# Layer 2 projections of a two-layer cross-attention packed to 320 columns, with high and low halves side by side in the third block

## The chip, the cores and the metric

The kernel runs on one core of a Trainium2 chip. The core has a matrix engine (PE, with its weight loads shown apart as PEld), a vector engine (DVE), a scalar engine (ACT), GpSimd (POOL), and SyncE (SP), which here issues nearly all transfers (DMAs). The metric is the device time of one execution in microseconds (us), lower is better. The kernel before has a median of 1475.77 us over 3 runs (1475.01 to 1476.06).

## The reference, cut to what matters

Two cross-attention layers run one after the other on 16 samples of 256 positions and 320 channels, with 20 heads of 16 channels. The context has 252 text positions used by layer 2 (77 by layer 1) and image tokens behind them. Layer 2 is this:

```python
q = heads(hidden_states @ W_q)
k_t = heads(text_ehs @ W_k)
v_t = heads(text_ehs @ W_v)
scores_t = jnp.einsum('bhsd,bhtd->bhst', q, k_t) * attn_scale
probs_t = jax.nn.softmax(scores_t, axis=-1)
...
k_ip = heads(ip_ehs @ W_k_ip)
attn_scores = jnp.einsum('bhsd,bhnd->bhsn', q, k_ip) * attn_scale
qsem = _l2norm(jnp.einsum('bhst,bte->bhse', probs_t, text_ehs))
fused = attn_scores + SEM_SCALE * jnp.einsum('bhse,bne->bhsn', qsem, ip_n)
probs_ip = jax.nn.softmax(fused, axis=-1) * spatial_mask[None, None, :, None]
out = (text_out + IP_SCALE * ip_out) @ W_out + b_out + residual
```

What is touched here is how `q`, `k_t` and `k_ip` of layer 2 are computed and how they reach the scores.

## The kernel before, in words

**Precision by halves.** A float32 value is held as a high half, rounded to the type that PE multiplies (`FR`), and a low half, the rest. A product is three matmuls per 128 rows of contraction: high by high, high by low, low by high (`prod`). Copies that make the high half are on ACT, the subtractions that make the low half on DVE or POOL (`halves`).

**Projections of layer 2.** `keys1(b)` computes the keys of sample b: the weights `w1["k"]` (tile wA) are 512 rows by `CP` = 384 columns, which are 16 channels of 24 heads, 4 of them padding; three blocks `m` of 128 columns are made, each by 12 matmuls of 252 moving columns (tile cta is the context). `queries(1, a)` does the same for the queries through `project` (weights in tile wE, input halves in tile hq): three blocks of 8 matmuls of 256 moving columns, fewer than nine since the contraction is 320 long and the last 64 rows of it carry high and low halves of the input side by side.

**The way to the scores.** The halves of the keys (tile kst) and of the queries (tile q) are written to DRAM, `kd` and `qd`, as three planes (low, high, high and high, low, high), so that one contraction over 48 rows (3 planes by 16 channels) gives the three products of a head's score. `stacks1(k)` reads them back per group of four heads as stacks of 48 rows (tiles ks and qs, two heads above one another at rows 0 and 64), with one further row of -1 against the row maxima. PE multiplies the stacks twice: L922 gives scores (tile S) for the maxima and L917 the transposed scores (tile T) that are exponentiated.

**Order.** The program is written as slots: 80 of layer 1 (five groups of four heads for each of 16 samples), then 80 of layer 2. `slot1(k)` has the transposed scores of group k, the scores of group k+2, the value product of k-2 (L988, L990), and the normalizing product of k-1 (`norm1`, L975: 14 matmuls of 512 moving columns, tiles ctb and gm). All else (projections, context loads, output) is cut into steps, and a table `STEPS` gives the due time of each in slots; `fill(now)` runs the steps that are due where a slot yields a number. In layer 2 the order of PE, ACT, DVE and POOL is the written one; SP's order of DMAs is set by a scheduler. Each engine works through its queue in order, so on SP a DMA that waits holds those behind it.

**Weights.** `weights7` loads the layer 2 key weights for text and image tokens, `weights2` the query weights, `weights8` clears a table in DRAM. They run during the last slots of layer 1.

The rows of the profile name tiles without numbers. The lines to follow: L260 and L632 (matmuls of the projections), L562 and L564 (key halves), L640 and L641 (query halves), L83 (every SP DMA), L917, L922 (scores), L975 (`norm1`).

```python
def slot1(k):
    yield lambda: both1(k, 1)
    if last:
        yield lambda: norm1(last, 0, 0)
    yield 0.2
    for parts in summed:
        yield lambda: settle1(*parts)
```

Of the kernel before, what the change touches and what calls it, by code (L numbers as in the profile page):

```python
# [16 lines left out]
B = 16  # L17
S = 256
H = 20
# [13 lines left out]
KS0 = 127  # L33
KS1 = 49
XROW = 48


# [12 lines left out]
def xattn2(  # L50
# [100 lines left out]

    kd = [dram.tile([B // 2, 3, CQ, 2, S], F32, name="kd0"), dram.tile([B, 3, CP, 1, S], F32, name="kd1")]
    vipd = dram.tile([BI, CP], F32, name="vipd")
# [79 lines left out]

    def weights(w_d, tag, half=None, wait=0, raw="raw"):

        w, parts, view = by_row(w_d, tag)
        yield from in_turn(parts, wait, raw)
        if half is not None:
            nc.vector.tensor_scalar_mul(w[:, 1, 2], f(w[:, 1, 2]), half)
        return view  # L240
# [14 lines left out]
    def prod(out, lhs, rhs, kt):  # L255

        terms = [(k, a, b) for k in range(kt) for a, b in ((0, 0), (0, 1), (1, 0))]
        first = last = None
        for i, (k, a, b) in enumerate(terms):
            last = mm(out, lhs(a, k), rhs(b, k), start=i == 0, stop=i == len(terms) - 1)  # L260
            first = first or last
        return first, last

    def context(b, n, wait=0):
# [94 lines left out]

    def last_keys(ct, kst, jobs):  # L360
# [119 lines left out]
    def weights7():  # L480
        cip = w1["cip"]
        image, wki1 = by_column(wki1_d)
        _, text, w1["k"] = by_row(wk1_d, "wA")
        yield from in_turn(image + text, 0.3, "rawc")
        for m in range(3):
            kp = bank()[:, :BI]
            prod(kp, lambda s, k: wki1(s, k, slice(m * 128, m * 128 + 128)), lambda s, k: cip[:, s, k], 4)
            halves(kip[:, 0, m], kip[:, 1, m], kp)
            yield
# [25 lines left out]
    def weights2():  # L515
        wq.append((yield from weights(wq1_d, "wE", tmask[:, 3:4], 0.3, "rawc")))

# [3 lines left out]
    def weights8():  # L521

        zero = buf("kb", [128, 3, 2, 96], FR, bufs=2, name="zero").rearrange("p a b c -> p (a b c)")
        nc.gpsimd.memset(f(zero), 0.0)
        yield
        for b in range(0, B, 4):
# [26 lines left out]
    def keys1(b):  # L553
        ct = ct1[b] = yield from context(b, 1, 0.3)
        for m in range(3):
# [7 lines left out]
            late(  # L563
                lambda kst=kst, kp=kp: nc.vector.tensor_sub(kst[:, 1, 0, :T1], kp, f(kst[:, 0, 0, :T1])),  # L564
                lambda kst=kst, m=m: keys_out(kd[1][b], m, kst),
            )
# [58 lines left out]

    def project(l, w, a, evac):

        terms = [(s, k, t) for k in range(2) for s, t in ((0, k), (0, 3 + k), (1, k))] + [(0, 2, 2), (1, 2, 2)]
        for m in range(3):
            pp = bank()[:, :S]  # L630
            for i, (s, k, t) in enumerate(terms):
                mm(pp, w(s, k, slice(m * 128, (m + 1) * 128)), a[:, t], start=i == 0, stop=i == len(terms) - 1)  # L632
            evac(m, pp)
            yield

    def queries(l, a):
# [5 lines left out]

        yield from project(l, wq[l], a, evac)
        qd = dram.tile([3, (CQ, CP)[l], S], F32, tag=f"qd{l}", name=f"qd{l}", bufs=2)
        settled()
        if l:
            for r, s in ((0, 0), (1, 1), (2, 0)):
                dma(qd[r].rearrange("(m p) t -> p m t", p=128), qh[:, s])
        else:
# [97 lines left out]
    def stacks1(k):  # L747
# [7 lines left out]
        for u in range(2):  # L755
            rows = slice(64 * u, 64 * u + XROW)
            hs = slice(4 * g + u, 4 * g + u + 3, 2)
            if k - NS < n:
                dma(K[64 * u + XROW : 64 * u + KS1], w1["ind"])
            dma(K[rows], stack_rows(kd[1][b][:, :, 0])[:, hs])  # L760
            dma(Q[rows], stack_rows(qd)[:, hs])

# [140 lines left out]
    def both1(k, t):  # L903
# [14 lines left out]
        if a:  # L918
            for j in range(2):
                for u in range(2):  # L920
                    rows = slice(64 * u, 64 * u + XROW)
                    mm(sp[:, 2 * u + j], a[0][rows, j, t * 128 : (t + 1) * 128], a[1][rows, j], start=True, stop=True)  # L922
# [28 lines left out]
    def maxima1(k):  # L951
# [5 lines left out]
        nc.scalar.copy(mt, mp[:4, :S])  # L957
        row = QK[k][0].rearrange("(u p) j t -> u p j t", u=2)[:, XROW]
        late(lambda: nc.scalar.dma_start(f(row), f(mt)))
# [33 lines left out]
    def slot1(k):  # L993
# [10 lines left out]
        yield release  # L1004
        yield lambda: both1(k, 1)
        if last:
            yield lambda: norm1(last, 0, 0)
        yield 0.2
        for parts in summed:
# [170 lines left out]
    def first_keys():  # L1180
# [5 lines left out]
    STEPS = {  # L1186
        "k1": (-7, -6.2, -6.2, -5, -4.2, -3.4,),
        "t1": (-3.2, -2.2, -2.2, -1.4, -0.2,),
        "o1": (-7, -6.8, -6, -5.8, -4, -3.4,),
        "i1": (6.8, 7.6, 7.6, 8.8, 9.4, 9.6, 10.6, 10.8, 10.8, 12.2,),  # L1190
        "c1": (12.8, 12.8, 13.4, 14, 14, 15.8,),
        ("i1", B - 2): (6.6, 7, 7.2, 7.2, 7.8, 8, 8.6, 9.2, 9.2, 9.6,),
        ("c1", B - 2): (9.8, 11.8, 11.8, 12.2, 12.4, 12.4,),
        ("i1", B - 1): (6.8, 7.6, 7.8, 10, 10, 10, 11, 11, 11.2, 12,),
        ("c1", B - 1): (12.2, 13, 13, 13.2, 13.4, 16,),
# [30 lines left out]
    }  # L1226
    def first(n, *key_times):
# [242 lines left out]
```

## Time and profile before

| what | before |
|---|---|
| median of the runs | 1475.77 us |
| the profiled execution, its own time | 1477.49 us |
| its span, first to last instruction | 1475.7 us |
| PE busy | 1433.6 us (97%) |
| PE weight loads busy | 1186.7 us (80%) |
| DVE busy | 1166.0 us (79%) |
| POOL busy | 1151.8 us (78%) |
| ACT busy | 956.5 us (65%) |
| PE clock granted, mean | 0.993 |

The profile is one execution. Its parts used here are the busy shares, the chain that ended last, the waits of PE, busy times in chosen stretches, and the instructions in order of time. An engine at 97% busy is not proof that it bounds the kernel, since the ends of matmuls are modelled; the distances from one matmul's start to the next one's start are recorded, and are the firmer reading.

### The profile page before, as it was taken

How to read it: one execution, taken by the hardware profiler on the slowest of the kernel's cores; microseconds unless marked ns; L12 is line 12 of the kernel's file. 1: busy time of each engine (PE TensorE's matmuls, PEld its weight loads, DVE VectorE, ACT ScalarE, POOL GpSimd, SP SyncE). 2: the span in 40 equal slices, each digit the busy share in tenths (PEclk: the TensorE clock that was granted, in tenths of full speed). 3: DMA queues.
4: the chain of work that ended last, by engine and by line, in shares of the span. 5: the costliest groups of instructions: out<-in, count | busy, mean ns of one | idle time of the engine just before them, and what ended most of it. 6: DMA issues, size and time to landing. Idle time of an engine off the chain costs nothing.

```text
span 1475.7 us, 35302 instructions
## 1 busy us (share of the span) xinstructions
PE 1433.6 (97%) x12438; PEld 1186.7 (80%) x12438; DVE 1166.0 (79%) x2569; ACT 956.5 (65%) x2074; POOL 1151.8 (78%) x1173
## 2 busy tenths in 40 slices
PE   6899999999999999799999999999999999999998
PEld 6788888888888878687778887888888888888865
DVE  5487676777677787967888888888888888888897
ACT  5577676767676776756666566656665666566553
POOL 4179797979797877987788877787778877887785
PEclk9999999999999999999999999999999999999999
DMA  6756565656656577565434433543354345433511
GB/s 196 194 160 184 134 184 141 184 143 165 162 154 164 144 195 205 140 184 158 138 102 140 146 119 101 161 146 102 118 161 146 89 131 161 135 101 116 150 32 50
DMA packets 230667, 211.78 MB, mean 144 GB/s; under 512 B 56314, under 2 KB 217116, under 8 KB 230492
## 3 DMA queue, kind: packets, MB, share of 16 engines
q1 hardware_dynamic: 229222, 208.56, 50.3%
q8 instruction: 99, 1.62, 0.5%
q10 hardware_dynamic: 1270, 0.98, 0.2%
q14 instruction: 76, 0.62, 0.1%
HBM read 122.07 MB, written 86.44 MB: 141 GB/s over the span
## 4 chain that ended last, share of the span: by engine, by line
PE 86%; DMA 4%; DVE 3%; POOL 3%; ACT 2%; issue 1%; SPq 0%; ACTq 0%; DVEq 0%; POOLq 0%
PE X L260 22%; PE X L975 18%; PE X L632 11%; PE P L833 7%; PE S L772 5%; PE P L988 5%; PE T L917 5%; PE T L795 4%; PE S L922 3%; PE P L990 2%; DMA kd<-kst 2%; PE X L1108 1%; POOL P L801 1%; PE X L690 1%; POOL wt L966 1%
## 5 line engine op out<-in xcount | busy, mean ns | idle before, releaser
L801 POOL TENSOR_TENSOR P<-P,rs 128x512 f32<-128x512 f32 x320 | 413.6, 1316 | 140.2 <-ACT P L798 140.2
L975 PE MATMUL X<-ctb,gm 128*128 128x512 f32 x1120 | 295.3, 407 | 0.0
L966 POOL TENSOR_TENSOR wt<-P,ctb 128x512 f32<-128x512 f32 x212 | 268.6, 1296 | 0.0
L923 DVE TENSOR_REDUCE mn<-S 128x4 fp32r<-128x1008 f32 x160 | 192.8, 1205 | 81.0 <-PE S L922 79.4
L975 PEld LDWEIGHTS X<-ctb,gm 128*128 128x128 f32 x1120 | 203.6, 190 | 49.4 <-issue 0.4
L798 ACT ACTIVATE P<-T 128x512 f32<-128x512 f32 x320 | 174.7, 593 | 100.5 <-PE T L795 81.0
L978 DVE TENSOR_TENSOR wt<-X,wt 128x512 f32<-128x512 f32 x240 | 159.3, 681 | 4.9 <-PE X L975 4.9
L929 ACT ACTIVATE P<-T 128x512 f32<-128x512 f32 x212 | 115.0, 597 | 54.5 <-PE T L917 41.6
L980 POOL TENSOR_TENSOR wt<-wt 128x512 f32<-128x512 f32 x80 | 103.6, 1295 | 58.3 <-DVE wt L978 58.3
L965 ACT ACTIVATE ctb<-P 128x512 fp32r<-128x512 f32 x212 | 122.5, 625 | 32.7 <-PE X L975 31.1
L774 DVE TENSOR_REDUCE mn<-S 128x4 fp32r<-128x716 f32 x160 | 142.4, 890 | 0.0
L833 PE MATMUL P<-P,vr 128*32 128x256 f32 x1920 | 123.8, 387 | 1.8 <-DVE tmp L850 0.8
L632 PE MATMUL X<-hq,wE 128*128 128x256 f32 x768 | 111.1, 289 | 4.4 <-ACT hq L615 3.9
L260 PE MATMUL X<-cta,wA 128*128 128x252 f32 (+3 forms) x726 | 104.2, 289 | 6.9 <-ACT wA L187 6.8
L632 PE MATMUL X<-ho,wF 128*128 128x256 f32 x768 | 106.6, 284 | 0.9 <-DVE ho L871 0.6
L632 PEld LDWEIGHTS X<-hq,wE 128*128 128x128 f32 x768 | 101.6, 195 | 7.2 <-ACT hq L615 4.4
L260 PEld LDWEIGHTS X<-cta,wA 128*128 128x128 f32 (+1 forms) x726 | 94.4, 191 | 10.7 <-ACT wA L187 7.0
L632 PEld LDWEIGHTS X<-ho,wF 128*128 128x128 f32 x768 | 98.7, 189 | 3.9 <-DVE ho L871 1.0
L844 DVE STREAM_TRANSPOSE nt<-P 128x512 f32<-128x512 f32 x80 | 57.0, 713 | 44.2 <-PE P L833 43.9
L773 DVE TENSOR_REDUCE mn<-S 128x4 fp32r<-128x308 f32 x160 | 74.5, 466 | 21.5 <-PE S L772 21.1
L833 PEld LDWEIGHTS P<-P,vr 128*32 128x32 f32 x1920 | 55.7, 110 | 42.7 <-issue 6.0
L772 PE MATMUL S<-ks,qs 125*128 125x256 f32 x480 | 87.0, 304 | 0.9 <-DVE mn L774 0.8
(223 smaller groups left out, 3279.7 us busy)
## 6 DMA issues: line engine op xcount, KB each, us to landing
qd<-q SPq DMA_DIRECT2D x48, 384.0 KB
kd<-kst SPq DMA_DIRECT2D x66, 256.0 KB
rawc<-in_cT_dram SPq DMA_DIRECT2D x60, 256.0 KB
qs<-qd SPq DMA_DIRECT2D x160, 96.0 KB
ks<-kd SPq DMA_DIRECT2D x160, 96.0 KB
qs<-qd SPq DMA_DIRECT2D x60, 192.0 KB
ks<-kd SPq DMA_DIRECT2D x60, 192.0 KB
qd<-q SPq DMA_DIRECT2D x32, 256.0 KB
```

The costliest lines, as they stand in the source:

```text
L260: last = mm(out, lhs(a, k), rhs(b, k), start=i == 0, stop=i == len(terms) - 1)
L632: mm(pp, w(s, k, slice(m * 128, (m + 1) * 128)), a[:, t], start=i == 0, stop=i == len(terms) - 1)
L772: mm(sp[:, h], Q[: XROW + T0, h, t * 128 : (t + 1) * 128], K[: XROW + T0, h], start=True, stop=True)
L774: anchor(nc.vector.tensor_reduce(mn[:, t, 1], sp[:, :, T0:], axis=AX.X, op=ALU.max))
L798: exp = anchor(nc.scalar.activation(pt, st[p], AF.Exp, scale=SCALE))
L801: anchor(nc.gpsimd.tensor_mul(pt, pt, rs[:, t : t + 1].to_broadcast([128, 2, S])))
L833: mm(pv[32 * s : 32 * s + 32, o : o + S], v[:, vt, h : h + 32], P[k, s // 2][:, t, s % 2], start=vt < 2, stop=vt != 1,)
L923: anchor(nc.vector.tensor_reduce(maxes[k + 2][:, t], sp[:, :, :T1], axis=AX.X, op=ALU.max))
L965: nc.scalar.activation(R[k, u][:, t], P[k, u][:, t], AF.Copy, scale=0.5)
L966: anchor(nc.gpsimd.tensor_sub(W[k, u][:, t], P[k, u][:, t], f(R[k, u][:, t])))
L975: mm(yp, gm[:, gb], R[k, u][:, kt], start=i == 0, stop=i == len(blocks[n]) - 1)
L978: nc.vector.tensor_mul(product, yp, w[:, n])
```

## The change

The layer 2 weights for keys, image keys and queries are packed to `CQ` = 320 columns (16 channels of 20 heads). Blocks 0 and 1 (256 columns) are computed as before. The third block has 64 columns left; the high halves of these weights fill its left 64 columns, and their low halves are copied beside them into the right 64 (`lows_beside`, on POOL). One matmul then gives both, so the third block takes 8 matmuls for keys (`both_halves`: context high and low) and 5 for queries, and the part that came from the low weights stands in rows 64 to 127 of the result as remainder rows.

The remainders are not added to the main rows. They enter the scores as further rows of the stacks: four rows in which the remainder of the query meets the main key, and four in which the main query meets the remainder of the key, so a stack has 56 rows (`X1`) in place of 48. The first of each four is only partly used (64 columns are 3.2 channels of 20 heads), and the unused parts in DRAM are cleared once, in `weights8`. The buffers `qd1` in DRAM become two fixed tensors.

For each sample the queries are now written by 7 DMAs (before 3) and the third key block by 4 (before 2). The image key weights come in four loads of 128 rows (before three loads of 128 columns). Further, `norm1(last, 0, 0)` moves behind the first `yield 0.2` of a slot, and due times in `STEPS` move by some tenths of a slot; the entries added for the last samples of layer 1 repeat what the default gave.

```diff
+    def lows_beside(w):
+        nc.gpsimd.tensor_copy(w[:, 0, :, CQ:], f(w[:, 1, :, LAST]))
...
+    def both_halves(out, lhs, rhs, kt):
+        for k in range(kt):
+            for s in range(2):
+                mm(out, lhs(k), rhs(s, k), start=k + s == 0, stop=k + s == kt)
...
+    def keys1_out(d, m, kst):
+        hi, lo = kst[:, 0, 0], kst[:, 1, 0]
+        n, lo_row = min(CQ - m * 128, 128), m * 128
+        planes = d[:EXTRA].rearrange("(r c) t -> c r t", c=CQ)[lo_row : lo_row + n]
+        dma(planes[:, 1:], hi[:n].unsqueeze(1).to_broadcast([n, 2, S]))
+        dma(planes[:, 0], lo[:n])
+        if m == 2:
+            dma(d[EXTRA + H - 4 : EXTRA + 4 * H], hi[:64])
+            dma(d[EXTRA + 5 * H - 4 : EXTRA + 8 * H], hi[64:])
...
-            prod(kp, lambda s, k: w1["k"](s, k, ms), lambda s, k: ct(s, k)[:, :T1], 4)
+            if m < 2:
+                prod(kp, lambda s, k: w1["k"](s, k, ms), lambda s, k: ct(s, k)[:, :T1], 4)
+            else:
+                both_halves(kp, lambda k: w1["k"](0, k, ms), lambda s, k: ct(s, k)[:, :T1], 4)
...
+            chain = [(0, k, t) for s, k, t in terms if s == 0] if beside and m == 2 else terms
...
             for r, s in ((0, 0), (1, 1), (2, 0)):
-                dma(qd[r].rearrange("(m p) t -> p m t", p=128), qh[:, s])
+                dma(planes[: 2 * 128, r].rearrange("(m p) t -> p m t", p=128), qh[:, s, :2])
+            dma(planes[LAST, ::2], qh[:64, 0, 2].unsqueeze(1).to_broadcast([64, 2, S]))
+            dma(planes[LAST, 1], qh[:64, 1, 2])
+            dma(qd[EXTRA + H - 4 : EXTRA + 4 * H], qh[64:, 0, 2])
+            dma(qd[EXTRA + 5 * H - 4 : EXTRA + 8 * H], qh[:64, 0, 2])
...
+        if last:
+            yield lambda: norm1(last, 0, 0)
-        yield 0.2
...
-        "k1": (-7, -6.2, -6.2, -5, -4.2, -3.4,),
+        "k1": (-7, -6.2, -6.2, -5.2, -4.2, -3.6,),
```

Two places show what this makes of the order. The first is PE in a slot of layer 2 in the middle of the program, between the scores of one slot and those of the next: the rows with cta,wA at 252 columns are the third key block, those with ctb,gm are `norm1`, those with wC,cta make values. Before:

```order
L922 MATMUL S<-ks_190,qs_186 128x256 x4
L975 MATMUL X<-ctb_82,gm 128x512 x7
L975 MATMUL X<-ctb_83,gm 128x512 x4
L260 MATMUL X<-cta_80,wA_84 128x252 x6
L260 MATMUL X<-cta_81,wA_84 128x252 x6
L975 MATMUL X<-ctb_83,gm 128x512 x3
L260 MATMUL X<-wC_155,cta_80 128x320 x6
L260 MATMUL X<-wC_155,cta_81 128x320 x6
L955 MATMUL X<-ident_r,mn_555 4x128 x2
```

And now:

```order
L969 MATMUL S<-ks_192,qs_188 128x256 x4
L1022 MATMUL X<-ctb_84,gm 128x512 x7
L279 MATMUL X<-cta_82,wA_86 128x252 x4
L279 MATMUL X<-cta_83,wA_86 128x252 x4
L1022 MATMUL X<-ctb_85,gm 128x512 x7
L271 MATMUL X<-wC_157,cta_82 128x320 x6
L271 MATMUL X<-wC_157,cta_83 128x320 x6
L1002 MATMUL X<-ident_r,mn_557 4x128 x2
```

Four matmuls are gone, and the third key block stands four matmuls of 512 columns further ahead.

The second is SP's queue for one sample, from the writes of its queries to the reads of its key stacks (qd and kd are the DRAM buffers; out_dram and xc belong to another sample's output). Before:

```order
L83 DMA out_dram<-xc_747 128x3x256
L83 DMA qd_12911<-q_297 128x3x256 x2
L83 DMA xc_747<-x1d 128x3x256
L83 DMA qd_12911<-q_297 128x3x256
L83 DMA kd_67<-kst_236 128x2x256
L83 DMA kd_67<-kst_236 128x256
L83 DMA qs_186<-qd_12911 48x2x256 x4
L83 DMA qs_187<-qd_12911 48x2x256 x2
L83 DMA kd_67<-kst_235 128x2x256
L83 DMA kd_67<-kst_235 128x256
L83 DMA qs_187<-qd_12911 48x2x256 x2
L83 DMA ks_190<-kd_67 48x2x256 x4
```

And now, where the writes of query blocks 0 and 1 (128x2x256, three of them) and the first of the third block (64x2x256) already stand ahead of these rows:

```order
L86 DMA qd_68<-q_299 64x256 x2
L86 DMA out_dram<-xc_749 128x3x256
L86 DMA qd_68<-q_299 64x256
L86 DMA kd_67<-kst_238 128x2x256
L86 DMA kd_67<-kst_238 128x256
L86 DMA xc_749<-x1d 128x3x256
L86 DMA qs_188<-qd_68 56x2x256 x4
L86 DMA qs_189<-qd_68 56x2x256 x2
L86 DMA kd_67<-kst_237 64x2x256
L86 DMA kd_67<-kst_237 64x256 x3
L86 DMA qs_189<-qd_68 56x2x256 x2
L86 DMA ks_192<-kd_67 56x2x256 x4
```

The last query write moved ahead of the load of xc, and the third key block has four writes instead of two between the query stacks and the key stacks.

More of the change, by code (lines that the diff above doesn't have):

```diff
@@ L33 @@
 KS0 = 127
-KS1 = 49
+KS1 = 57
 XROW = 48
+X1 = 56
+LAST = slice(2 * 128, CQ)
+EXTRA = 3 * CQ
 SIZES = dict(RAW=2, KST=2, NP=4, NR=4, CTA=2, CTB=2, WB=4, M=2)
@@ L150, in const_tile @@
         return const.tile(shape, dtype, tag=tag, name=tag)
-    kd = [dram.tile([B // 2, 3, CQ, 2, S], F32, name="kd0"), dram.tile([B, 3, CP, 1, S], F32, name="kd1")]
+    kd = [dram.tile([B // 2, 3, CQ, 2, S], F32, name="kd0"), dram.tile([B, X1 * H, S], F32, name="kd1")]
+    qd1 = [dram.tile([X1 * H, S], F32, name=f"qd1{i}") for i in range(2)]
     vipd = dram.tile([BI, CP], F32, name="vipd")
@@ L232, in by_column, with weights @@
         )
-    def weights(w_d, tag, half=None, wait=0, raw="raw"):
-        w, parts, view = by_row(w_d, tag)
+    def lows_beside(w):
+        nc.gpsimd.tensor_copy(w[:, 0, :, CQ:], f(w[:, 1, :, LAST]))
+    def weights(w_d, tag, half=None, wait=0, raw="raw", beside=False):
+        w, parts, view = by_row(w_d, tag, beside)
         yield from in_turn(parts, wait, raw)
         if half is not None:
-            nc.vector.tensor_scalar_mul(w[:, 1, 2], f(w[:, 1, 2]), half)
+            n = CQ if beside else CP
+            nc.vector.tensor_scalar_mul(w[:, 1, 2, :n], f(w[:, 1, 2, :n]), half)
+        if beside:
+            lows_beside(w)
         return view
@@ L515, in weights2 @@
     def weights2():
-        wq.append((yield from weights(wq1_d, "wE", tmask[:, 3:4], 0.3, "rawc")))
+        wq.append((yield from weights(wq1_d, "wE", tmask[:, 3:4], 0.3, "rawc", True)))
     def weights4(l):
@@ L524, in weights8 @@
         nc.gpsimd.memset(f(zero), 0.0)
+        blank = zero[:16, :S].unsqueeze(1)
+        for d in (*(q.unsqueeze(0) for q in qd1), kd[1]):
+            for row in (EXTRA, EXTRA + 4 * H):
+                dma(d[:, row : row + 16].rearrange("b p t -> p b t"), blank.to_broadcast([16, d.shape[0], S]))
         yield
@@ L624, in split, with project @@
         return hl
-    def project(l, w, a, evac):
+    def project(l, w, a, evac, beside=False):
         terms = [(s, k, t) for k in range(2) for s, t in ((0, k), (0, 3 + k), (1, k))] + [(0, 2, 2), (1, 2, 2)]
@@ L630, in project @@
             pp = bank()[:, :S]
-            for i, (s, k, t) in enumerate(terms):
-                mm(pp, w(s, k, slice(m * 128, (m + 1) * 128)), a[:, t], start=i == 0, stop=i == len(terms) - 1)
+            chain = [(0, k, t) for s, k, t in terms if s == 0] if beside and m == 2 else terms
+            for i, (s, k, t) in enumerate(chain):
+                mm(pp, w(s, k, slice(m * 128, (m + 1) * 128)), a[:, t], start=i == 0, stop=i == len(chain) - 1)
             evac(m, pp)
             yield
+    opened = []
     def queries(l, a):
```

47 lines of the change are left out of this document (31 added, 16 removed), and 24 rows, old and new, of the table STEPS.

## The prediction

> **What bounds the kernel now.** I read the page's busy shares first, then its chain that ended last, then PE's waits in layer 2, then PE row by row.
>
> ```profile
> PE 1433.6 (97%) x12438; PEld 1186.7 (80%) x12438; DVE 1166.0 (79%) x2569; ACT 956.5 (65%) x2074; POOL 1151.8 (78%) x1173
> PE 86%; DMA 4%; DVE 3%; POOL 3%; ACT 2%; issue 1%; SPq 0%; ACTq 0%; DVEq 0%; POOLq 0%
> ```
>
> PE is 97% busy and 86% of the chain. Since a busy PE can still be a slow one, the next rows matter more: stretches in us, each with the busy us (and instructions) of PE, PEld, DVE, ACT and POOL, then granted clock, DMA share and GB/s. The first is one sample of layer 2 (49.65 us, from one read of the same table to the next), the second the slot in it with the third key block; then come all waits of PE between 760 and 1440 us.
>
> ```profile
> 1001.30:1050.95 49.65, 49.65 (x419) 40.23 (x418) 42.55 (x90) 30.88 (x68) 39.46 (x44) 1.00 0.43 129
> 1028.10:1035.49 7.39, 7.39 (x53) 6.45 (x50) 6.84 (x15) 4.04 (x9) 5.38 (x9) 1.00 0.72 228
> ```
>
> ```profile
> PE P L990 <- DVE wt L980: 1.1, 1, 1.1
> PE S L922 <- DVE sr L939: 0.9, 2, 0.7
> ```
>
> In 680 us PE waits 2.0 us. DVE has 42.55 of 49.65 us, POOL 39.46. PE in order of time (start, us, group) says whether it runs at its own pace:
>
> ```profile
> 1011.08 1.11 PE L632 MATMUL X<-hq,wE 128*128 128x256 f32 x8
> 1012.03 2.49 PE L975 MATMUL X<-ctb,gm 128*128 128x512 f32 x10
> ...
> 1028.10 0.40 PE L922 MATMUL S<-ks,qs 48*128 48x256 f32 x4
> 1028.43 2.83 PE L975 MATMUL X<-ctb,gm 128*128 128x512 f32 x11
> 1031.10 1.55 PE L260 MATMUL X<-cta,wA 128*128 128x252 f32 x12
> 1032.48 0.86 PE L975 MATMUL X<-ctb,gm 128*128 128x512 f32 x3
> ...
> 1035.49 0.41 PE L922 MATMUL S<-ks,qs 48*128 48x256 f32 x4
> ```
>
> From start to start, 11 matmuls of 512 columns take 2.67 us (243 ns each), 12 of 252 columns 1.38 us (115 ns), 8 of 256 columns 0.95 us (119 ns). The time goes with the columns, there is no gap between groups, and so a matmul taken out of layer 2 gives back its own start-to-start time, as long as no other engine steps in.
>
> **The removed matmuls.** Each of 16 samples loses 4 of 252 columns and 3 of 256: 4 x 0.115 + 3 x 0.119 = 0.817 us, so 13.1 us in all. The other price for the same instructions is busy time by group:
>
> ```profile
> L632 PE MATMUL X<-hq,wE 128*128 128x256 f32 x768 | 111.1, 289 | 4.4 <-ACT hq L615 3.9 <-DVE hq L616 0.3
> L260 PE MATMUL X<-cta,wA 128*128 128x252 f32 x576 | 75.8, 279 | 0.2 <-POOL cta L188 0.2
> ```
>
> 111.1/768 = 145 ns and 75.8/576 = 132 ns, which make 0.96 us a sample and 15.4 us. I take 13.1, since busy time counts the tails of matmuls that overlap the next group; 15.4 is the upper end.
>
> By the Trainium skill (TensorE: Matmul & The Clock Gate, Back-to-back issue gap) an isolated matmul takes N/2.4 + 2.5 ns, which as an estimate makes 12.1 us here; the same section's sustained figure of about 131 ns at 512 columns would make the rest cheaper still, near 11 us. The 243 ns above contradict that sustained figure, and the trace stands.
>
> The score matmuls contract 56 or 57 rows instead of 48 or 49. Their moving columns stay 256, and the rows above show that 48 contracted rows take 0.33 us for four (1028.10 to 1028.43) with two heads above one another; 57 rows still fit into the same 64. Cost nothing.
>
> **The moved norm1 and steps.** These reorder PE work without changing it. What could be lost is cover. In the slot of the third key block DVE is busy 6.84 of 7.39 us; the slot shrinks by 4 x 0.115 = 0.46 us to 6.93, so DVE still fits with 0.09 us to spare. DVE at the end of that slot (start, us, group, and in brackets the idle time before):
>
> ```profile
> 1035.11 0.44 DVE L1100 STREAM_TRANSPOSE rs<-rs 128x256 f32<-128x256 f32 x1
> 1035.93 1.21 DVE L923 TENSOR_REDUCE mn<-S 128x4 fp32r<-128x1008 f32 x1 [0.38 <-PE S L922]
> ```
>
> DVE idles 0.38 us there and then reduces the scores; behind this reduction waits the next write of S on PE, the half of the scores about 2.1 us on, and the reduction needs 1.21 of these. So a DVE that is 0.1 us late holds nobody. If that cover were gone in full, the loss is bounded by the saving of that slot: 16 x 0.46 = 7.4 us. I take 0.
>
> **DMAs.** A sample issues 46 DMAs on SP in place of 40 (queries 7 for 3, third key block 4 for 2), and the stacks carry 56 rows for 48. Bytes have room: the DMA share in the sample's row is 0.43. What counts is the time at which the first key stacks of the next sample land. SP (start, us for all issues of the row):
>
> ```profile
> 1029.58 0.36 SPq L83 DMA_DIRECT2D xc<-x1d  x1
> 1030.03 0.44 SPq L83 DMA_DIRECT2D qd<-q  x1
> 1030.57 1.45 SPq L83 DMA_DIRECT2D kd<-kst  x2
> 1034.40 2.82 SPq L83 DMA_DIRECT2D qs<-qd  x6
> 1037.33 0.89 SPq L83 DMA_DIRECT2D kd<-kst  x2
> ...
> 1040.69 4.06 SPq L83 DMA_DIRECT2D ks<-kd  x8
> 1044.85 0.38 SPq L83 DMA_DIRECT2D sid<-sr  x1
> 1046.85 1.83 SPq L83 DMA_DIRECT2D si<-sid  x4
> ```
>
> ```profile
> 1046.06 0.51 PE L922 MATMUL S<-ks,qs 48*128 48x256 f32 x4
> ```
>
> Key block 3 is written at 1037.33 and 1037.8; the read waits until 1040.69, about 2.9 us from issue to landing. The two reads for the first group are issued by about 1041.1 and so should land by 1044.0, and the scores that need them start at 1046.06: 2.1 us of slack. The two added writes cost 0.45 us each (0.89/2), 0.9 us. Against that, the block is multiplied earlier on PE (4 x 0.243 + 0.46 = 1.4 us), and the chain ahead is shorter: the six query reads wait until 1034.40 for the query write of 1030.03, which itself stood behind the load of xc and goes ahead of it now. So the key reads stay roughly where they are, and the scores come 0.8 us earlier in each sample. I take 0; the bounds are 0 and the late-stacks rival.
>
> **Weights and the change of layers.** DVE makes the low halves of narrower weights, POOL gets two copies more:
>
> ```profile
> L188 DVE TENSOR_TENSOR wA<-rawc,wA 128x384 fp32r<-128x384 f32 x4 | 3.5, 873 | 0.0
> L188 DVE TENSOR_TENSOR wA<-P,wA 128x320 fp32r<-128x320 f32 x4 | 1.9, 486 | 1.1 <-ACT wA L187 1.1
> L304 POOL CAST wA<-wB 128x64 fp32r<-128x64 f32 x8 | 2.4, 319 | 1.9 <-ACT wB L187 1.4 <-DVE wB L188 0.5
> ```
>
> For wA DVE saves between 4 x 0.15 us (873 x 64/384) and 4 x 0.39; the POOL copies (256 and 192 elements) cost between 0.32 us and four times that each. All of it lies beside other work in the last slots of layer 1, as do the six clearing DMAs. How much PE idles between 560 and 760 us, and its clock when it stumbles there, bounds what a new order can win or lose:
>
> ```profile
> 680.00:700.00 20.00, 18.70 (x132) 15.09 (x131) 14.31 (x29) 10.64 (x23) 11.10 (x14) 0.91 0.46 149
> ...
> sum 200.00, PE 188.76 PEld 153.32 DVE 158.49 ACT 127.50 POOL 160.00; mean PE 18.88 PEld 15.33 DVE 15.85 ACT 12.75 POOL 16.00
> ```
>
> ```profile
> 682.83 0.50 PE L922 MATMUL S<-ks,qs 48*128 48x256 f32 x4 [0.79 <-DVE sr L939]
> 683.26 5.08 PE L975 MATMUL X<-ctb,gm 128*128 128x512 f32 x14
> 688.17 0.28 PE L955 MATMUL X<-ident_r,mn 128*4 128x128 f32 x2
> ```
>
> PE idles 11.2 us there. After two short waits the granted clock falls to 0.91 of a 20 us stretch, and 14 matmuls take 4.91 us where 14 x 0.243 = 3.4 would do: 1.5 us lost in such a spell. A new order could win or lose about half of the idle time, so 6 us either way; no row says which, and I take 0.
>
> **The sum.** -13.1 us. Against the profiled execution's own 1477.49 us (span 1475.7 and 1.8 around it) that is 1464.4; that execution lies 1.7 us above the median of the runs, and from the median 1475.77 it is 1462.7 us, 0.9% less.
>
> **Rivals.**
>
> *The shorter slots are taken over by another engine.* DVE keeps 0.09 us in the slot of the third key block by its busy sum, and moving norm1 behind the 0.2 steps delays its first product on DVE. For it: 6.84 of 7.39 us. Against it: the 0.38 us of idle time, and the next slot's slack. It would take the 7.4 us of the keys and leave 5.7: 1470.1.
>
> *More than the sum: the change of layers runs better.* For it: 11.2 us of idle time and slow-clock spells to be won. Against it: nothing in the change shortens what PE waited for there except a few DVE operations. -13.1 - 6: 1456.7.
>
> *The key stacks land late (slower).* If all six added issues stood in series ahead of the first key read, it would move by 6 x 0.45 = 2.7 us, 0.6 more than the slack, in each of 15 samples: 9 us, which alone gives 1471.7. But such a wait can bring the slow clock, as at 683 us, with 1.5 us each time: 15 x 2.1 = 31.5, so 1494. It ends slower than before once a sample loses more than 0.87 us in both ways together (13.1/15). For it: the issues are serial on SP, and 2.1 us is the whole slack. Against it: four of the six lie where SP waits anyhow (nothing is issued between 1032.0 and 1034.40). By the Trainium skill (the same page, HAM oscillation — how this bites in real kernels) waits beyond about 3.4 us in every round bring a half-rate clock in every round; the 0.91 above would be such a half rate for 3.4 of 20 us, but it came after waits of under 1 us. The skill's page on transfers (DMA: Bandwidth & Descriptors, Bandwidth) calls transfers under 64 KB descriptor-dominated; the added ones lie at that edge (64 rows of 1 KB), and no run here shows what that costs.
>
> *Nothing measurable.* The change of layers loses 6 us by its new order, and the keys lose their 7.4: 1475.8 - 13.1 + 13.4 = 1476.1.
>
> **How the numbers follow.** The sum as it stands: 0.67, from 1458.7 to 1466.7 with some 4 us for the change of layers. Taken over by DVE: 0.11. Better than the sum: 0.08. Late stacks: 0.10. Nothing measurable: 0.04. Within 0.2% (3 us, about what a measurement tells from no change) is the last case; faster are the first three, 0.86; slower 0.10. The range of 1457 to 1470 holds the first case, nearly all of the third and half of the second.
>
> **What the profile after would show.** If right: one sample of layer 2 takes about 48.8 us in place of 49.65; PE stays at 100% between 760 and 1400 us with waits of a few us in total; the third key block takes 0.92 us and the hq,wE group 0.6 us, at 115 and 119 ns per matmul; no wait of S or T on a DMA of ks or qs; DVE about 87% busy per sample. Wrong: S waiting on ks<-kd or on DVE sr once per sample, granted clock below 1.00 in the middle of layer 2, or more than 17 us of idle PE between 560 and 760 us.

## The result and the profile after

The changed kernel takes 1478.80 us (median of 12 runs, 1475.22 to 1482.69) against 1476.52 us (12 runs, 1473.66 to 1481.76) of the kernel before: ratio 1.0016, 95% interval [1.0003, 1.0029]. It is 0.2% slower, the edge of what can be told from no change, where 0.9% faster was forecast. Its profiled execution took 1479.14 us with a span of 1477.4.

The page of the changed kernel, busy shares and the chain that ended last:

```profile
PE 1421.9 (96%) x12326; PEld 1172.4 (79%) x12326; DVE 1170.0 (79%) x2571; ACT 958.2 (65%) x2075; POOL 1147.7 (78%) x1175
PE 76%; DVE 7%; DMA 7%; POOL 3%; ACT 3%; issue 2%; SPq 2%; ACTq 0%; DVEq 0%; POOLq 0%
```

112 matmuls and 11.7 us of PE's busy time are gone, and the span is no shorter: PE's share of the chain fell from 86% to 76%, and DMA, DVE and SP's queue took it. Stretches of the changed kernel (us; busy us and instructions of PE, PEld, DVE, ACT, POOL; granted clock, DMA share, GB/s), and the first of them in the kernel before under it:

```profile
400.00:600.00 200.00, 189.25 (x1732) 163.73 (x1736) 141.87 (x337) 137.62 (x302) 153.09 (x137) 0.97 0.63 167
1000.00:1100.00 100.00, 100.00 (x837) 80.97 (x836) 87.86 (x185) 63.61 (x137) 79.97 (x88) 1.00 0.48 139
```

```profile
400.00:600.00 200.00, 194.73 (x1822) 168.27 (x1821) 151.62 (x357) 144.50 (x316) 163.36 (x143) 0.99 0.65 176
```

Between 400 and 600 us the changed kernel gets 90 matmuls less done, before the layer that was changed has begun (slot 80, at 674 us of before). Where the time goes is seen best slot by slot. This table gives how much later ACT's first exponential of a slot starts than in the trace of before (us, worked out from the starts of these rows; slot 66 is at 576 us of before, and 90 to 155 are 13 samples of layer 2):

| slot | 60 | 63 | 65 | 66 | 90 | 155 | end |
|---|---|---|---|---|---|---|---|
| changed kernel | +0.2 | +2.7 | +11.9 | +9.6 | +12.2 | +3.7 | +1.7 |

In layer 2 it gains 8.5 us in 13 samples, about 0.65 each. What it gains there it has lost ahead of it: 12 us between slots 60 and 90, and 9.2 of these in one place, of which slot 66 gives 2.3 back. The longest of PE's waits between 545 and 590 us, and then PE and ACT in order of time around it (in brackets the idle time before, and what ended it):

```profile
PE P L880 <- ACT P L845: 6.8, 1, 6.8
```

```profile
563.69 2.78 PE L271 MATMUL X<-kst,wB 128*128 128x64 f32 x24
573.31 2.79 PE L880 MATMUL P<-P,vr 128*32 128x256 f32 x24 [6.84 <-ACT P L845]
576.03 1.22 PE L819 MATMUL S<-ksl,qsl 125*128 125x256 f32 x4
577.05 1.05 PE L842 MATMUL T<-qs,ks 127*128 127x256 f32 x4
577.90 0.48 PE L756 MATMUL X<-ident,sp 128*77 128x128 f32 x2
```

```profile
562.28 0.78 ACT L791 CAST ks<-M 77x716 fp32r<-77x716 f32 x1
571.84 0.62 ACTq L830 DMA_DIRECT2D qs<-mt  x1
572.57 1.09 ACT L845 ACTIVATE P<-T 128x512 f32<-128x512 f32 x2 [9.50 <-DMA qs<-qd]
```

PE waits 6.84 us for an exponential of ACT. ACT waits 9.50 us, and not with the exponential itself: ahead of it in ACT's queue stands the DMA that writes the row of maxima (mt) into a query stack, and this DMA is held until 571.84 us. In the kernel before the same DMA goes at once:

```profile
559.63 0.78 ACT L744 CAST ks<-M 77x716 fp32r<-77x716 f32 x1
559.93 0.62 ACTq L783 DMA_DIRECT2D qs<-mt  x1
560.65 1.08 ACT L798 ACTIVATE P<-T 128x512 f32<-128x512 f32 x2 [0.24 <-ACT ks L744]
```

After the wait PE runs slowly as well. Between 560 and 580 us it got a clock of 0.74; the trace has it at half from 567.86 to 578.10 us:

```profile
560.00:580.00 20.00, 13.16 (x111) 11.40 (x110) 7.70 (x18) 6.82 (x16) 6.66 (x8) 0.74 0.89 255
```

From 573.31 to 578.14 it took 4.83 us for work that takes half of that at full clock. 6.84 + 2.4 = 9.2 us, the jump from slot 63 to slot 65. The rule of the Trainium skill (TensorE: Matmul & The Clock Gate, HAM oscillation — how this bites in real kernels) that PE gaps beyond some 3.4 us bring a slow clock fits this wait of 6.84 us. It does not cover all that the traces show: in the kernel before, the clock stood at half from 683.48 to 686.89 us behind waits of 0.51 and 0.79 us.

The chain, in order of time (start, us, what), shows what held the DMA:

```profile
564.44 7.33 DMA qs<-qd
...
571.84 0.62 ACTq L830
```

It is the load of another query stack on SP's queue, issued at 564.44 and landed at 571.77. The maxima row needs nothing of that load. In the kernel before the same load took as long, from its issue at 560.58 to its landing at 567.95, and held nobody. SP's queue at this time (start, us for the issues of the row):

```profile
555.42 0.81 SPq L86 DMA_DIRECT2D kd<-kb  x2
556.28 2.07 SPq L86 DMA_DIRECT2D qd<-kb  x1
558.45 2.64 SPq L86 DMA_DIRECT2D x1d<-xc  x1
561.13 0.49 SPq L86 DMA_DIRECT2D qd<-kb  x1
561.67 1.57 SPq L86 DMA_DIRECT2D spread_d<-kb  x2
563.34 1.05 SPq L86 DMA_DIRECT2D ks<-kd  x1
564.44 1.25 SPq L86 DMA_DIRECT2D qs<-qd  x1
565.79 1.19 SPq L86 DMA_DIRECT2D xc<-in_xT_dram  x1
567.02 0.61 SPq L86 DMA_DIRECT2D spread_d<-kb  x1
567.68 0.68 SPq L86 DMA_DIRECT2D rawc<-in_wv_dram  x1
568.40 0.64 SPq L86 DMA_DIRECT2D spread_d<-kb  x1
569.13 1.19 SPq L86 DMA_DIRECT2D rawc<-in_wv_dram  x1
570.37 0.95 SPq L86 DMA_DIRECT2D qd<-kb  x2
```

Four of the six new clears (two of 256 KB, kd<-kb, and two of 16 KB, qd<-kb) and two clears of 768 KB that the kernel before had too (spread_d<-kb) stand ahead of that load; all six new ones lie within these rows. And the load is the eighth DMA ahead of the maxima row's in the order in which the program was written: the load, xc, a clear, weights, a clear, weights and two clears are eight (in the trace both report on the same semaphore). The DMAs of this program report their completion on eight semaphores in turn, over SP's and ACT's queues together, and each waits until the DMA that had its semaphore before has landed. The theory is that the six clears cause the wait through this count: they delay the landing of the eighth DMA ahead (the load was issued 3.9 us later than before), and they shift which DMA that is (theory A; some expectations still put it by bytes). The rivals are that traffic or issues ahead in the queue are what costs, and, apart from the clears, that the new order of the steps loses the time or that the removed matmuls were never worth 13 us.

### The profile page after: what moved, and what is told of

Read it like the earlier page. It is cut to its first block, busy times and chain, and to the rows that moved or that the text cites. A ratio compares the mean times of both kernels' runs of the same rounds, so it can differ in the third digit from the quotient of the medians.

```text
span 1477.4 us, 35267 instructions
## 1 busy us (share of the span) xinstructions
PE 1421.9 (96%) x12326; PEld 1172.4 (79%) x12326; DVE 1170.0 (79%) x2571; ACT 958.2 (65%) x2075; POOL 1147.7 (78%) x1175
## 4 chain that ended last, share of the span: by engine, by line
PE 76%; DVE 7%; DMA 7%; POOL 3%; ACT 3%; issue 2%; SPq 2%; ACTq 0%; DVEq 0%; POOLq 0%
PE X L271 18%; PE X L1022 15%; PE X L671 10%; PE P L880 6%; PE S L819 5%; PE P L1035 4%; PE T L842 4%; PE T L964 4%; PE S L969 2%; DMA kd<-kst 2%; PE P L1037 2%; SPq L86 2%; POOL P L848 2%; DVE wt L1025 1%; DMA qs<-qd 1%
## 5 line engine op out<-in xcount | busy, mean ns | idle before, releaser
L1022 PE MATMUL X<-ctb,gm 128*128 128x512 f32 x1120 | 289.7, 403 | 0.0
L671 PE MATMUL X<-ho,wF 128*128 128x256 f32 x768 | 110.4, 287 | 3.7 <-DVE ho L920 1.8
L671 PE MATMUL X<-hq,wE 128*128 128x256 f32 x720 | 104.6, 288 | 4.9 <-ACT hq L653 3.4
L671 PEld LDWEIGHTS X<-hq,wE 128*128 128x128 f32 x720 | 93.9, 193 | 8.0 <-ACT hq L653 3.9
L819 PEld LDWEIGHTS S<-ks,qs 125*128 125x128 f32 x480 | 65.4, 191 | 26.3 <-issue 22.9
L842 PE MATMUL T<-qs,ks 127*128 127x256 f32 x480 | 79.7, 289 | 6.5 <-DMA qs<-mt 4.4
```

Source lines behind the costliest of these rows:

```text
L819: mm(sp[:, h], Q[: XROW + T0, h, t * 128 : (t + 1) * 128], K[: XROW + T0, h], start=True, stop=True)
L842: mm(st[p][:, j], K[:KS0, 2 * p + j, t * 128 : (t + 1) * 128], Q[:KS0, 2 * p + j], start=True, stop=True)
L1022: mm(yp, gm[:, gb], R[k, u][:, kt], start=i == 0, stop=i == len(blocks[n]) - 1)
```

## The experiments

Ratios are against runs of the kernel before on the same chip; line numbers are those of each kernel.

**The clears added to the kernel before (e2).** Six DMAs of the shapes of the clears, into a buffer that nothing reads; the order of PE, ACT, DVE and POOL stays that of before.

```diff
+    spare = [dram.tile([n, 1120, S], F32, name=f"spare{i}") for i, n in enumerate((1, 1, B))]
...
+        blank = zero[:16, :S].unsqueeze(1)
+        for d in spare:
+            for row in (960, 1040):
+                dma(d[:, row : row + 16].rearrange("b p t -> p b t"), blank.to_broadcast([16, d.shape[0], S]))
```

> The kernel before with six further DMAs of the same shapes as the clears, into DRAM that nothing reads, issued by the same step; nothing else. Theory A, clears: a wait of PE of several us near 560 to 575 us appears, and the time is 8 to 12 us above before, 1484 to 1488. Theory B, table: no more than 2 us above before, since the engines' orders are those of before.

1484.01 us, ratio 1.0047 [1.0027, 1.0067], so about 7 us slower: less than the 8 to 12 us that were expected, and far from the 2 us at most of the rival. The slots up to 63 are unmoved (-0.7 us), and from 66 on all lag 6.5 to 6.7. The longest wait of ACT and that of PE, 545 to 590 us:

```profile
ACT P L803 <- DMA spare<-kb: 10.2, 1, 10.2
```

```profile
PE P L838 <- ACT P L803: 7.6, 1, 7.6
```

The exponential waits for a write that no instruction reads. So the clears alone make this wait, and no dependence of data is behind it.

**Two of them, the large ones (e7).** The same, with `for d in spare[2:]`: the two writes of 256 KB, nearly all of the bytes.

> The kernel before, with only the two DMAs of 256 KB from 16 partitions at that place. Theory A (traffic): the two carry nearly all of the bytes, so 4 to 8 us slower than before, and ACT or PE wait several us on one of them near 565 us. Rival B (count of issues): a third of the six, 1 to 3 us slower. A third reading, C: what decides is which DMA of the turn the row of maxima meets, so that two fewer or four fewer issues shift it onto another one: then the time is near that of before although the traffic is there.

1476.24 us, ratio 1.0005 [0.9994, 1.0016]: nothing, which only the third reading had as possible. The maxima row's DMA started at 560.70, 0.08 us behind the end of x1d<-xc at 560.62. That store is now the eighth ahead, and it was issued ahead of the writes of 256 KB. The bytes alone don't cost the time.

**Six small ones (e6).** The same count and place as in e2, 16 KB each.

```diff
+        blank = zero[:16, :S].unsqueeze(1)
+        for d in spare:
+            for row in (960, 1040):
+                dma(d[0, row : row + 16], blank[:, 0])
```

> The kernel before, with six more DMAs at the same place as in the run with the six clears, but each of them writes only 16 rows of 1 KB. Theory A (it is the traffic of the two clears of 256 KB, some 2.8 us each to land, that holds up the DMAs behind them and those that share their completion semaphores): within 2 us of the kernel before, and no wait of ACT of more than 1 us near 565 us. Rival B (six more issues are enough, through SP's time of about 0.5 us each and the turn of the completion semaphores): 5 to 8 us slower, like the run with the large clears.

1479.63 us, ratio 1.0028 [1.0016, 1.0039], about 4 us slower, with one wait of ACT for a DMA near 565 us:

```profile
ACT P L803 <- DMA spare<-kb: 5.4, 1, 5.4
```

Theory A, put by bytes in this expectation, said no wait; its rival said 5 to 8 us slower. Neither range holds. The wait comes with 96 KB too, and is shorter since what stands eight places ahead lands sooner (564.95 us, in e2 569.11).

**Five that stand behind (e11).** The sharpest test: five writes of 8 KB that SP issues behind the load of the query stack, so that they can't delay it, but that stand ahead of the maxima row's DMA in the program's order. The order of all other engines is that of before.

```diff
+    spare = dram.tile([5, 128, 2, 2, 4], F32, name="spare")
...
+        for i in range(5 if k == 66 else 0):
+            dma(spare[i], mn)
         mt = buf("mt", [8, S], FR)
```

In the built programs the maxima row's DMA of that slot reads as follows (DMAHW0 to DMAHW7 are the eight completion semaphores), in the kernel before, in e7 and in this one:

```
L783 DMA qs2_188<-mt_0_196 2x4x256 [waits DMAHW2_49,Activation_49]
L788 DMA qs2_191<-mt_0_199 2x4x256 [waits DMAHW4_49,Activation_49]
L786 DMA qs2_189<-mt_0_197 2x4x256 [waits DMAHW7_49,Activation_49]
```

> The kernel before, with five DMAs of 8 KB (the row maxima of one slot, which nothing reads) that stand in SP's queue behind the load of the query stack issued at 560.58 us in the profile of before. In the program's order they stand ahead of ACT's DMA of the maxima row that went at 559.93 us, so that this DMA comes eighth behind the query stack's load instead of eighth behind a clear of the spread buffer. Theory A (a DMA waits until the one eight places ahead of it in the program's order has landed, whatever it carries): ACT's DMA goes at about 568.0 us, within 0.2 us behind the landing of that load, ACT waits some 7 to 8 us there, and the kernel is 4 to 9 us slower. Rival B (the loss comes from bytes or issues that stand ahead in the queue): these stand behind, 40 KB in all, so ACT's DMA goes at 559.9 us and the time is that of before, within 2 us.

1481.78 us, ratio 1.0039 [1.0026, 1.0051], about 6 us slower. SP, ACT and the chain:

```profile
558.93 1.27 SPq L83 DMA_DIRECT2D qs<-qd  x1
560.30 3.25 SPq L83 DMA_DIRECT2D spare<-mn  x5
```

```profile
565.90 0.62 ACTq L786 DMA_DIRECT2D qs<-mt  x1
566.62 1.09 ACT L801 ACTIVATE P<-T 128x512 f32<-128x512 f32 x2 [7.71 <-DMA qs<-qd]
```

```profile
558.93 6.89 DMA qs<-qd
```

The wait is 7.71 us where 7 to 8 were expected, and the DMA starts 0.08 us behind the landing of the load that by count now stands eighth ahead. The start came 2.1 us ahead of the expected 568.0, as the load landed sooner. What the DMA waits for follows from its place in the count, not from bytes or issues ahead of it. All cases together (us in each kernel's own trace):

| kernel | eighth DMA ahead | landed | maxima row's DMA starts |
|---|---|---|---|
| before | second clear of spread_d | 559.86 | 559.93 |
| changed | load of a query stack | 571.77 | 571.84 |
| e2 | write into spare, issued at 560.40 | 569.11 | 569.19 |
| e6 | third small write into spare | 564.95 | 565.02 |
| e7 | store of x1d | 560.62 | 560.70 |
| e11 | load of a query stack | 565.82 | 565.90 |

Also in the kernel before this DMA had such a predecessor; it just landed in time.

**The clears moved ahead (e1).** The changed kernel, with the six clears issued one by one from slot 20 of layer 1 on, from a zero tile of their own.

```diff
+    blank16 = const_tile([16, S], "blank16")
...
-        blank = zero[:16, :S].unsqueeze(1)
-        for d in (*(q.unsqueeze(0) for q in qd1), kd[1]):
-            for row in (EXTRA, EXTRA + 4 * H):
-                dma(d[:, row : row + 16].rearrange("b p t -> p b t"), blank.to_broadcast([16, d.shape[0], S]))
...
+    task(("w9",), [-60 + NS + 2.1 * i for i in range(7)], weights9)
```

> The changed kernel with the six clearing DMAs issued around slot 20 of layer 1, where the profile shows PE at 99.7%, from a zero tile of their own; all else as in the changed kernel. Theory A, clears: in the changed kernel they stand ahead of a stack load on SP near 560 us, ACT waits 9.5 us for that load, and 9 to 12 us go there; without them the wait at 560 to 575 us is gone and the time is 1467 to 1470 us, 0.5% or more below before. Theory B, table: the new due times and the fourth image weight load make the wait; then it stays and the time is 1476 us or more.

1468.18 us, ratio 0.9939 [0.9915, 0.9963], as theory A had it. Against the changed kernel's 1.0016 the clears' place is worth 0.0077, or 11.4 us. In the two traces, which end 12.8 us apart, 9.1 of these arise between slots 63 and 66, where the wait was, and 2.2 in the 13 samples of layer 2, most of it at the output projection (below). The stretch around the former wait:

```profile
560.00:580.00 20.00, 20.00 (x193) 18.13 (x191) 13.95 (x36) 12.50 (x29) 15.22 (x15) 1.00 0.75 190
```

PE doesn't wait, and its clock is full.

**All clears moved ahead (e8).** As e1, with the four clears of the spread buffer ahead too (`range(11)` steps instead of 7).

> The changed kernel with the six clears and also the four clears of 768 KB of the score stacks' spread buffer moved ahead to layer 1. Theory A (whatever clears stand in SP's queue at the change of layers delay the stacks behind them): another 1 to 5 us faster than with the six alone, 1463 to 1467 us. Rival B (those four were on nobody's path once the six are gone): 1468 us, within 2. If they now disturb layer 1, more than 1470 us.

1480.14 us, ratio 1.0029 [1.0015, 1.0043]: the gain is lost again, which only the last line of what was expected allowed for. Slot 20 lags 1.3 us, slot 25 9.8. The longest single waits of ACT and PE between 180 and 300 us:

```profile
ACT P L853 <- DMA kd<-kst: 8.6, 1, 8.6
```

```profile
PE T L850 <- ACT P L853: 6.2, 1, 6.2
```

It is the same wait in layer 1: the maxima row's DMA starts at 242.98, 0.08 us behind the landing at 242.90 of a key write that the clears had delayed. So it isn't the change of layers that makes the wait, but DMAs that land late among the eight ahead of one that ACT issues; by e6 and e7 their size alone doesn't decide. The 8.5 us between slots 20 and 25 are not the whole of the some 13 us between e1 and e8, and the rest was not followed.

**The matmuls alone (e3).** The kernel before, without the seven matmuls of a sample, so the low halves of the third block's weights are not multiplied.

```diff
-            prod(kp, lambda s, k: w1["k"](s, k, ms), lambda s, k: ct(s, k)[:, :T1], 4)
+            if m < 2:
+                prod(kp, lambda s, k: w1["k"](s, k, ms), lambda s, k: ct(s, k)[:, :T1], 4)
+            else:
+                for k in range(4):
+                    for s in range(2):
+                        mm(kp, w1["k"](0, k, ms), ct(s, k)[:, :T1], start=k + s == 0, stop=k + s == 4)
...
+            chain = [x for x in terms if x[0] == 0] if beside and m == 2 else terms
```

> The kernel before with the seven matmuls per sample left out of the third blocks (low halves of the weights there are not multiplied, so a part of each product is missing) and nothing else. By the price of the prediction (115 and 119 ns each) 13.1 us less, 1463 to 1464 us. If instead another engine takes over in the shortened slots, 1468 or more; if PE were not the bound, 1476.

1464.68 us, ratio 0.9913 [0.9893, 0.9933], 12.8 us. The interval, 9.9 to 15.8 us, would hold the price by busy time too; the slots are finer, 10.5 us in 13 samples or 0.81 each, where 0.82 was forecast and busy time makes 0.96. The price of the matmuls holds.

**The order of the steps (e4, e5, e9, e10).** e4 is the changed kernel with the table of steps and the place of norm1's first part of before.

```diff
-        yield 0.2
         if last:
             yield lambda: norm1(last, 0, 0)
+        yield 0.2
...
-        "k1": (-7, -6.2, -6.2, -5.2, -4.2, -3.6,),
+        "k1": (-7, -6.2, -6.2, -5, -4.2, -3.4,),
...
-        ("q0", B - 2): tuple(NS + x for x in (-21.8, -21, -20, -19, -18,)),
...
```

In the diff of the change, ahead of the prediction, these signs stand the other way round; as its text says, the changed kernel has the pause (`yield 0.2`) first and norm1 behind it.

> The changed kernel with the due times of before and norm1 ahead of the 0.2 steps again. Theory A, clears: the wait near 560 us stays, 1476 to 1483 us. Theory B, table: the wait goes, and the time is 1464 to 1468 us.

1471.80 us, ratio 0.9957 [0.9941, 0.9973], between what the two theories had said. By its trace the maxima row's DMA waited for another predecessor, a key stack's load that landed at 563.30, and slot 66 lags 2.8 us instead of 9.6. Undoing the order had moved the clears in the queue too, so this run mixes two causes. The next three keep the clears early. e5 is e1 with table and norm1 of before, e9 is e1 with only norm1 back, e10 is e1 with only the table back.

> The changed kernel with its six clearing DMAs moved ahead to about slot 20 of layer 1, and with the table of steps and the place of the first norm that the kernel before had. Theory A (the clears alone cost the time, the order of the steps nothing): as with the new table, 1468.2 us, within 2 us of it. Rival B (the new table itself loses time behind slot 64, where the kernel with early clears gave back some 3 us that the old table did not): about 1464 to 1466 us, near the 1464.7 us of the kernel before without the seven matmuls. If the old table is worse once the clears are gone (rival C), over 1470 us.

> The changed kernel with the six clears early, and the first part of the first norm back at its place of before, ahead of the pause; the table of steps stays the new one. Theory A (the some 3 us between the early-clears kernels with the new and with the old order come from the norm's place): about 1464.4 us. Theory B (they come from the table of steps): about 1468 us. If both lie within 1466 to 1467 us, each has a part.

> The changed kernel with the six clears early, and the old table of steps; the first part of the norm stays at its new place, behind the pause. Theory A (the norm's place costs the some 3 us): about 1468 us. Theory B (the table costs them): about 1464.4 us.

| ratio, median | norm1 ahead of the pause, as before | norm1 behind it, as changed |
|---|---|---|
| old table | e5: 0.9926 [0.9910, 0.9942], 1464.39 | e10: 0.9957 [0.9941, 0.9973], 1470.36 |
| new table | e9: 0.9914 [0.9898, 0.9930], 1464.20 | e1: 0.9939 [0.9915, 0.9963], 1468.18 |

e5 came out as its rival B, e9 and e10 nearer to the theory that norm1's place costs. In both rows it does, 4.6 and 3.7 us (0.0031 and 0.0025 of 1476). The intervals of a row touch or overlap a little; that both rows and the traces agree carries it. The new table costs nothing in total and may gain some 2 us. By the slots this is a gain of 3.5 to 4.0 us in 13 samples of layer 2 and a loss of 2.4 to 5.0 us between slots 60 and 90. Groups of PE by line with count, busy us and mean ns, for 800 to 1400 us, with norm1 back (e9) and without (e1), and then one instance of each in order of time:

```profile
L677 PE MATMUL X<-ho,wF 128*128 128x256 f32 x304 | 41.6, 286 | 0.0
```

```profile
L677 PE MATMUL X<-ho,wF 128*128 128x256 f32 x304 | 44.1, 290 | 0.7 <-DVE ho L926 0.5
```

```profile
953.88 2.12 PE L677 MATMUL X<-ho,wF 128*128 128x256 f32 x16
```

```profile
953.01 0.92 PE L677 MATMUL X<-ho,wF 128*128 128x256 f32 x6
954.12 1.46 PE L677 MATMUL X<-ho,wF 128*128 128x256 f32 x10 [0.19 <-DVE ho L926]
```

The output projection multiplies ho. In the groups of 16 the first six matmuls find their part of ho ready, and the seventh waits for the part that DVE writes last (L926). From start to start the sixth takes 272 ns on average in e1 where it takes 118 in e9, and the seventh 214 where it takes 120, in 13 groups within 600 us; in e10 they take 267 and 213, in e5 119 and 120. In the changed kernel itself they take 395 and 222, which makes 1.7 of the 2.2 us that its layer 2 loses against e1's. Between e9 and e1 that is (154 + 94) x 13 = 3.2 us in some 12 samples, about 4 in 16. Most of these waits hardly show in the busy time, which has PE at 599.30 of 600 us, since the time of a matmul in it (290 ns) is longer than the distance to the next one.

norm1 doesn't write ho itself; what its place changes is the order on DVE. One instruction there, the third part of the halves of hq (L662), comes ahead of the write of ho, and it takes much longer (count, busy us and mean ns, 800 to 1400 us, in e9 and e1):

```profile
L662 DVE SCALAR_TENSOR_TENSOR hq<-hq,tmask,xq 128x256 fp32r<-128x256 f32 x12 | 7.6, 631 | 0.0
```

```profile
L662 DVE SCALAR_TENSOR_TENSOR hq<-hq,tmask,xq 128x256 fp32r<-128x256 f32 x12 | 17.2, 1432 | 0.0
```

One instance in e9 and in e1, beside the instruction of POOL that works on the same tile:

```profile
950.75 1.30 POOL L660 TENSOR_TENSOR hq<-xq,hq 128x512 fp32r<-128x512 f32 x1 [2.81 <-ACT hq L659]
...
951.41 0.92 DVE L662 SCALAR_TENSOR_TENSOR hq<-hq,tmask,xq 128x256 fp32r<-128x256 f32 x1
```

```profile
949.59 1.63 DVE L662 SCALAR_TENSOR_TENSOR hq<-hq,tmask,xq 128x256 fp32r<-128x256 f32 x1
949.64 1.30 POOL L660 TENSOR_TENSOR hq<-xq,hq 128x512 fp32r<-128x512 f32 x1 [2.61 <-ACT hq L659]
```

With norm1 ahead of the pause three short instructions stand between norm1's product and this one; with norm1 behind it they don't, so DVE comes to it about when POOL begins. In both instances it ends 0.28 us behind POOL's, and so it does in all 36 of e1, e10 and the changed kernel. Its mean is 1.41 to 1.50 us in these three and 0.48 to 0.63 in the kernel before, e3, e5 and e9. That it ends with POOL's instruction is what the traces show; why, no run tested.

e9, at 0.9914, is the fastest kernel of the study that leaves nothing out (e5 is not told apart from it): 12.7 us faster than before and, by the two ratios, 15.1 us faster than the changed kernel.

## Why the prediction was wrong

**The matmuls**, -13.1 us: right. e3 measured -12.8, and by its slots 0.81 us a sample. Pricing by start-to-start time held, and the 15.4 from busy time was too much. That e9, which has the whole change but for two things, comes to -12.7 is in part luck: by its slots it gains 1.1 us a sample and loses 3.8 us ahead of slot 90.

**The change of layers**, 0 and at most 6 either way: this step failed. Its sentence was that the weights' work lies beside other work, "as do the six clearing DMAs". By e1 they cost 11.4 us. I had asked which engine is busy beside them, and not who waits for SP's queue: the six were never followed in it, though the key writes of a sample in layer 2 were, issue by issue. The bound was of the wrong kind as well. Half of PE's idle time between 560 and 760 us says what stood there, not what a new wait may add; idle time in this stretch rose from 11.2 to 20.8 us. The mark for a wrong prediction, more than 17 us idle there, was met.

**The moved norm1**, 0 and at most 7.4: the second step that failed, by 3.7 to 4.6 us. It said that a DVE 0.1 us late holds nobody, since the reduction of the scores has room. It looked only at the slot of the third key block. In the slot of the output projection the new place lets DVE's hq instruction run beside POOL's and take 0.8 us longer, and the consumer that waits is not the scores but the output projection, which reads ho at its seventh matmul.

The sum -12.7 + 3.7 + 11.4 = +2.4 us is what 1.0016 of 1476 makes, but it must be so, since the terms are the differences between e9, e1 and the changed kernel. What bears each term out is e3 for the first and the waits in the traces for the others.

**The DMAs of a sample**, 0: right. The three largest of the six waits of PE between 760 and 1440 us in the changed kernel (the others make 1.0 us):

```profile
PE X L671 <- DVE ho L920: 1.8, 7, 0.3
PE S L969 <- DVE sr L986: 1.5, 4, 0.7
PE P L1037 <- DVE wt L1027: 1.1, 1, 1.1
```

No wait for ks or qs stands among the six, and the rival of late key stacks did not come. The first row is the wait for ho as far as single waits show it. DVE, at 87.86 of 100 us, is the 87% that was forecast; the rival in which DVE takes over the slot did not come in its place, the scores, but in another.

**"Nothing measurable"**, chance 0.04, came near the right time, and by luck: its two losses, 6 and 7.4 us, measured 11.4 and 3.7 and were placed half right, one at the change of layers, though not by a new order, and one that was DVE's, though not in the keys' slot.

The kernels with norm1 back differ in their slots (e9 lags 4.0 us at slot 90 and then gains 1.1 us a sample, e5 leads by 2.9 and gains 0.8), while their ends lie 2.5 us apart in the traces. In layer 2 the start-to-start times show most of it: between 800 and 1400 us the matmuls of cta by wA take 115.0 ns in e9 and 119.8 in e5 (384 of them), the transposed scores T 87.7 and 92.7 (some 497), against 86.7 and 78.2 for the 124 transposes of mn. That makes 3.3 us, or 0.27 a sample. Where e9 loses the 3.8 us ahead of slot 90 stays open.

## What to carry to other kernels

Count the DMAs that a change adds ahead of any DMA issued by a compute engine: in this program such a DMA waits for the eighth one ahead of it in the order of the program, on whatever queue, and the engine's next instruction waits with it; where that one lands late, a few small added DMAs are enough. Price a setup DMA at the place where it is issued, and if nothing needs it until later, issue it in a stretch in which no such engine issues one, then look at the waits there. Where a step is moved, see on every engine what comes to run beside what, compare how long the same instruction takes before and after, and follow what it delays down to the single matmul, since waits of 0.1 to 0.15 us hardly show in busy time and still made about 4 us here.

## What was not expected of the hardware

- Eight completion semaphores for SP's and ACT's DMAs: in every case of the table above a DMA started 0.07 to 0.08 us behind the landing of an unrelated one, also where that one writes a buffer that nothing reads (10.2 us of waiting). The waits stand in the built programs, as the three lines of e11 show; no run here shows whether the chip needs them.
- A write of 256 KB from 16 partitions is slow for its bytes. In the changed kernel the two clears landed at 559.78 and 562.59, 2.8 us apart, or 93 GB/s with little else under way, while the DMA rate was 255 GB/s in the mean of 560 to 580 us. What makes it slow was not tested.
- SP's issues can stretch: in the changed kernel 0.4 to 0.5 us each at 555.42 and 561.13, 1.0 to 2.6 us in most rows between 556 and 567 us, while the clears were under way (DMA share 0.89 between 560 and 580 us).
- An instruction of DVE (L662, hq) that takes 0.49 us in the mean of the kernel before took 1.3 to 1.6 us where it began within 0.3 us of an instruction of POOL on the same tile, and ended 0.28 us behind it each time.
